# A hybrid transformer block on one core: the V products of softmax attention taken one key tile at a time, with two exp buffers and a 4 KB descriptor scratch

## The chip, the core and the metric

The kernel runs on one NeuronCore of a Trainium2 chip. The core has five engines, each with its own queue that is worked in order: TensorE (PE, the matrix multiplier, fed from SBUF and writing to PSUM), VectorE (DVE), ScalarE (ACT), GpSimd (POOL) and SyncE (SP, which here issues DMAs only). They meet through semaphores. The metric is the device time of the whole program in microseconds (us); lower is better. The bound used for "faster", "same" and "slower" is 0.2% of the time before, 7.4 us.

## The reference

The input x has 8 sequences of 512 tokens and 1024 channels. Four blocks follow one another, each on the layer-normed x and added back to x:

- softmax attention with 32 heads of 32 channels: q, k, v from one 1024x3072 weight, scores of all 512x512 token pairs per head, softmax over the keys, times v, then a 1024x1024 output product;
- a dense layer of 1024x1024 whose output is masked by a query mask and a row mask, both from a softmax over 64 cluster centroids;
- causal attention with a sigmoid in place of the softmax, 4 heads of 256 channels;
- the same masked dense layer again.

```python
scores = jnp.einsum('bhqd,bhkd->bhqk', q, k) * scale
probs = jax.nn.softmax(scores, axis=-1)
ctx = jnp.einsum('bhqk,bhkd->bhqd', probs, v)
```

All is float32. The change touches the first block alone.

## The kernel before

Everything is in one program whose order was written out by hand: each engine works its instructions in the order in which the Python code emits them, and the tile framework adds only the semaphore waits that the data need.

**Units.** The first block is worked in 64 units. Unit n is one sequence (n // 8) and one group of four heads (n % 8): four heads of 32 channels fill 128 partitions. For each unit the kernel needs q and k (128 channels x 512 tokens), v (4 key tiles of 128 tokens x 128 channels), the maximum of each score row, exp of the shifted scores, their sum over the keys, the products with v, and a division.

**The loop** (lines 1039 to 1107) has four steps, i = 0 to 3, for each unit n, and does in each step work for three units at once:

- `rows_step(n + 1, i)` (line 895): scores of the next unit with the queries on the partitions, into the four-bank PSUM tile `sc`, and a DVE reduction for the row maxima (L906);
- `between()` (line 986): filler, see below;
- in step 0 `turn_max(n)`: the maxima are turned with matmuls (`tpm`);
- `keys_step(n, i)` (line 928): scores of unit n for key tile i with the keys on the partitions, again into `sc`, preceded by a product with ones that puts the shift in (L934, L937), and then exp by ACT into the SBUF tile `pT` (L939);
- `values_step` (line 952): the products of `pT` with v, added up over the four key tiles in the PSUM tile `av` (L961). Before the change one call does two key tiles: the call for tiles 0 and 1 stands in step 2 after `keys_step(n, 2)`, the call for tiles 2 and 3 stands in step 0 of the next unit after `keys_step(n + 1, 0)`;
- in step 0, after that, `normalize(n - 1)` (line 965): the matmul `den` (L973) adds the exp sums over the partitions, DVE turns, inverts and multiplies (L976 to L981), ACT adds the bias (L982);
- `sum_step` (line 942): the sum of `pT` over the key tiles. POOL adds tiles 0 and 1 after the exp of tile 1 (L948, two instructions); DVE adds tile 2 in step 3, before `keys_step(n, 3)`, and tile 3 in step 0 of the next unit, behind the reduction (L950);
- a second `between(False, ...)`.

**Buffers around the change.** `sc` has one buffer, so rows and keys take turns in it: a `rows_step` waits for the exp before it, a `keys_step` for the reduction before it. `av` has one buffer, which the L981 of the unit before must have read. The small PSUM tiles `mm` (which also hold `den`, `tpm` and `logitsT`) have three. `pT` has three buffers of 8 KB a partition (pool `a_pt`, line 439): the exp of a key tile waits until the tile three before it has been read by its V products and by its sum.

**Filler.** The q, k and v projections of unit n + 2, the output products of an earlier sequence and the dense layer's cluster products are cut into pieces and queued; `Filler.take` (line 115) runs a share of the queue at each `between`, by the weights in `FILLER_SHARES` (line 39): three shares in step 0 (0.5, 0.5, 0.6), two in each of steps 1 to 3 (1.0 and 1.0; 0.6 to 1.0). What is left is run at the end of the unit (`filler.until`, line 1107). V products aren't filler and don't enter the shares. DVE gets side tasks (layer-norm statistics, sums for the fast matrix products: L241, L612, L752, L991, L1377) at the same places.

**Column form of the filler.** `product` (line 574) cuts each 128-column product into `P // width[0]` matmuls on neighbouring column groups of the array, two of 64 columns or four of 32, which run side by side. `between` sets the width with its second argument (line 993), and it holds until the next `between`. Filler after a `values_step` runs with 32 columns (the form of the V products), all other filler of the loop with 64. In the profile a matmul's form is written as rows\*columns of the array that it uses: 128\*64, 128\*32; the score products are 32\*64 (rows) and 32\*128 (keys). An fp32 matmul shows as two records.

**DMA.** SP issues the weight loads (six buffers of 256 KB, refilled as they are used). POOL issues the stores of intermediate results (188 DMAs in all). Their descriptors are kept in an SBUF scratch, whose size the program's constructor takes (line 1716); where nothing is said it is 16 KB a partition.

Of the kernel before, what the change touches and what calls it, by code (L numbers as in the profile page):

```python
# [26 lines left out]
TPB = S // P  # L27
NTILE = NT // P

HEADS_A, HD_A = 32, 32  # L30
GH = P // HD_A
# [42 lines left out]
class Filler:  # L74
# [47 lines left out]
    def run(self, count):  # L122

        while self.queue and count:
            count -= self._run_one() > 0
# [295 lines left out]
def softmax_attention(tc, cst, stage, filler, clusters, pools, dr, late, args):  # L421
# [11 lines left out]
    nc, small, ps_m = tc.nc, stage.small, stage.ps_m  # L433
    outer, inner = pools
# [1 line left out]
    fixed, ctxp, rpool, npool = outer("a_fixed", 1), outer("a_ctx", 2), outer("a_r", 3), outer("a_n", 1)  # L436
    owpool, csp, xTp, sump = outer("a_ow", OW_BUFS), outer("a_cs", 1), inner("a_xT", 2), inner("a_sum", 1)
    wpool, xpool = inner("a_w", W_BUFS), inner("a_x", 2)
    qkpool, vpool, ptp, tmp = inner("a_qk", 3), inner("a_v", 5), inner("a_pt", 3), inner("a_tmp", 1)
    shiftp, ps_s, ps_a = inner("a_shift", 2), inner("a_ps_s", 1, PSUM), inner("a_ps_a", 1, PSUM)  # L440

    qkvb_s = fixed.tile([P, 3 * NC], F32, name="qkvb_s")
# [7 lines left out]
    units, half = B * NC, NC // 2  # L450
# [220 lines left out]
    def left_tasks(b):  # L671

        xT = xTs[b]
        a11, a12, a21, a22 = (xT[:, ts(k, half), ts(m, 2 * P)] for m in range(2) for k in range(2))
        sums = (sump.tile([P, half, 2 * P], F32, tag=f"s{k}", name=f"s{k}_{b}") for k in (1, 2, 4))
        lefts[b], steps = left_sums(nc, a11, a12, a21, a22, *sums)
        return [lambda: run(enumerate(steps[:2])), *steps[2:]]
# [60 lines left out]
    def ow_sum_tasks(c):  # L738

        st = {}  # L740

        def load():
            for name in ("B11", "B12", "B21", "B22"):
                st[name] = owpool.tile([P, S], F32, tag="ow", name=f"ow_{name}_{c}")
                nc.sync.dma_start(st[name], ow_source(name, c))

        def step(k):
            if k == 0:
                t = [csp.tile([P, half, P], F32, tag=f"c{m}", name="cbox").rearrange("p c t -> p (c t)") for m in range(4)]
                st["t"] = (t[0], t[1], t[3], t[2])  # L750
                st["steps"] = right_sums(nc, st["B11"], st["B12"], st["B21"], st["B22"], *t)
            st["steps"][k]()  # L752
            nc.gpsimd.dma_start(dr.osums[("T1", "T2", "T4", "T3")[k]][:, ts(c, S)], st["t"][k])

        return load, [partial(step, k) for k in range(4)]
# [139 lines left out]
    def rows_step(n, qt):  # L895

        st = state[n]
        if qt == 0:
            st["nmax"] = small.tile([P, TPB, GH], F32, tag="nmax", name=f"nmax_{n}")
        sc = ps_s.tile([P, GH, S], F32, tag="sc", name="sc")  # L900
        for h in range(GH):
            rows = ts(h, HD_A)
            for j in range(2):
                cols = ts(2 * qt + j, P // 2)
                nc.tensor.matmul(sc[ts(j, P // 2), h, :], st["q"][rows, cols], st["k"][rows, :], start=True, stop=True)  # L905
        nc.vector.tensor_reduce(st["nmax"][:, qt, :], sc, AX.X, ALU.max, negate=True)  # L906
# [11 lines left out]
    def turn_max(n):  # L918

        st = state[n]  # L920
        tp = ps_m.tile([P, TPB, P], F32, tag="mm", name="tpm")
        for qt in range(TPB):
            part = parts[n % 2][:, qt, :, :].rearrange("p h c -> p (h c)")
            product(tp[:, qt, :], part, cst.ident_h, start=True, stop=True)
        st["shift"] = shiftp.tile([P, S], BF16, tag="shift", name=f"shift_{n}")
        nc.scalar.copy(st["shift"], tp.rearrange("p t q -> p (t q)"))
# [15 lines left out]
    def sum_step(n, kt):  # L942

        st = state[n]
        if kt == 1:
            st["sum"] = tmp.tile([P, GH, S], F32, tag="sum", name="sum")
            for h in (slice(0, GH // 2), slice(GH // 2, GH)):
                nc.gpsimd.tensor_tensor(st["sum"][:, h, :], st["pT", 0][:, h, :], st["pT", 1][:, h, :], ALU.add)  # L948
        else:
            nc.vector.tensor_tensor(st["sum"], st["sum"], st["pT", kt], ALU.add)  # L950

    def values_step(n, k):

        st = state[n]
        if k == 0:
            st["av"] = ps_a.tile([P, S], F32, tag="av", name="av")
        for kt in (2 * k, 2 * k + 1):
            pT = st.pop(("pT", kt))
            for h in range(GH):
                rows = ts(h, HD_A)  # L960
                nc.tensor.matmul(  # L961
                    st["av"][rows, :], st["v"][:, kt, rows], pT[:, h, :], start=(kt == 0), stop=(kt == TPB - 1)
                )

    def normalize(n):

# [19 lines left out]
    def between(sides=True, form=2 * HD_A):  # L986


        if sides:
            for _ in range(-(-len(side) // places[0])):  # L990
                side.popleft()()  # L991
            places[0] -= 1
        width[0] = form
        filler.take()

    def mix_tile(near, wait):
        norm, logits = tiles.popleft()(blocks=wait)
        filler.mix(norm[:2], 0 if near else 2, 2 if near else 5)
        filler.mix(norm[2:], 9 if near else 14, 3)
        if wait:  # L1000
            waiting.append(logits)
        elif near:
            filler.mix(logits[:1], 16, 4)
            carried.extend(logits[1:])
        else:
            filler.mix(logits, 22, 4)

    def weave(pieces, products):

        out, at = [], 0  # L1010
        for j, product in enumerate(products):
            upto = 2 * round(len(pieces) * (j + 1) / (len(products) + 1) / 2)
            out += pieces[at:upto] + product
            at = upto
        return out + pieces[at:]
# [23 lines left out]
    for n in range(units):  # L1039
        b, g = divmod(n, NC)  # L1040
        ahead = n + 2
        if n == NC - 2:
            weights.fill(W_BUFS)
        if n == NC:
            run(next(outs))
            ows.fill(OW_BUFS)
        count = 0
        if n > NC:
            count = OUT_SHARES[(n - 1) % half] if n <= units - NC else LAST_SHARES[n - units]
        products = [next(outs) for _ in range(count)]  # L1050
        if ahead < units:
            if g == NC - 2:
                side.extendleft(reversed(left_tasks(b + 1)))
            filler.add(weave(project_pieces(ahead), products), mark=ahead)
        else:
            filler.add(weave([], products))
        ready.extend(waiting)
        waiting.clear()
        if tiles:
            mix_tile(n == units - 1, ahead < units)  # L1060
        side.extend(ow_later)
        ow_later.clear()
        if n == NC - 1:
            side.extend(last_sums)
        for c in OUT_SUMS.get(n, ()):
            load, steps = ow_sum_tasks(c)
            side.append(load)
            (ow_later if c == 0 else side).extend(steps)
        if b + 1 < B:
            if g == 0:  # L1070
                norms = deque(norm_tasks(b + 1))
            if g < 2:
                run(enumerate(norms.popleft()))
            if norms:
                side.extend(norms.popleft())
        side.extend(held)
        held.clear()
        filler.plan(FILLER_SHARES)
        places[0] = TPB + 1
        for i in range(TPB):  # L1080
            if n + 1 < units:
                rows_step(n + 1, i)
            if i == 0 and n > 0:
                sum_step(n - 1, TPB - 1)
            between()
            if i == 0:
                turn_max(n)
                between()
            if i == TPB - 1:
                sum_step(n, i - 1)  # L1090
            keys_step(n, i)
            if i == 1:
                sum_step(n, i)
            if i == 0 and n > 0:
                values_step(n - 1, 1)
                if ready:
                    by_cluster, by_token = ready.popleft()
                    run([by_cluster])
                    filler.mix([by_token], 6, 1)
                normalize(n - 1)  # L1100
            if i == 2:
                values_step(n, 0)
            between(False, HD_A if i in (0, 2) and n > 0 else 2 * HD_A)
        if n + 1 < units:
            split_max(n + 1)
        if ahead < units:
            filler.until(ahead)
# [3 lines left out]
    tiles.clear()  # L1111
    run(ready[0][0][:1])
    del ready[0][0][0]
    values_step(units - 1, 1)
    normalize(units - 1)
    yield
    spare = Slices(ctxp.tile([P, NC, S], F32, tag="ctxT", name="spare").rearrange("p c t -> p (c t)"))
# [607 lines left out]
```

## Time and profile before

| | |
|---|---|
| time, median of 3 runs | 3715.86 us (3714.45 to 3716.66) |
| the profiled execution, from the first to the last instruction | 3715.1 us, 0.8 us (0.02%) under that median |
| mean granted TensorE clock | 0.999 |
| PE busy | 3677.4 us, 99% |
| DVE busy | 2539.7 us, 68% |
| ACT busy | 927.8 us, 25% |
| POOL busy | 594.9 us, 16% |
| the 64 units | 72.7 to about 2521 us of the span |
| HBM traffic | 160 GB/s over the span |

A busy share is a union of intervals, and the ends of matmuls are modelled from a pipeline, so a PE that is 99% busy can still lose time between two forms of matmul or in a wait that is shorter than the pipeline's tail. The starts of the records are the safer guide: where two stretches of matmuls start tells how long the first took. In a timeline line the columns are the start in us from the span's start, the length in us, the engine, the source line, the operation, output<-inputs, the form and output size, the number of records merged, and in brackets how long the engine had been idle and what ended that.

### The profile page before, as it was taken

The page shows a single profiled execution, that of the slowest core. Times are in us where ns is not written, and L with a number is a line of the kernel's source. Part 1 is how long each engine was busy: PE and PEld are TensorE (multiplying, and loading weights), DVE is VectorE, ACT ScalarE, POOL GpSimd, SP SyncE. Part 2 cuts the span into 40 slices and gives each one's busy share as a digit, 9 for nine tenths or more (in the row PEclk, how much of TensorE's full clock was granted, in tenths as well). Part 3 has the DMA queues.
Part 4 walks back from the last instruction along what each step waited for, and adds up shares of the span by engine and source line. Part 5 has one row for each costly group of instructions (what it writes and reads, how often), then busy time and mean ns, then how long its engine had stood idle before and what let it go on. Part 6 is the DMA issues. An engine that isn't in the chain of part 4 may idle for free.

```text
span 3715.1 us, 76365 instructions
## 1 busy us (share of the span) xinstructions
PE 3677.4 (99%) x32792; PEld 1876.7 (51%) x32792; DVE 2539.7 (68%) x3497; ACT 927.8 (25%) x1017; POOL 594.9 (16%) x574
## 2 busy tenths in 40 slices
PE   8999999999999999999999999999999999999999
PEld 4444544544545455445445445444444467774444
DVE  4777676767667677766767767666788845556656
ACT  1222222222222222222222222222111144430000
POOL 1222111111111111111111111111000044530000
PEclk9999999999999999999999999999999999999999
DMA  5335444645655555465465454347566767763332
GB/s 184 113 122 179 142 143 147 192 138 157 185 153 150 159 162 163 133 198 152 139 182 159 143 150 124 122 156 244 158 180 179 184 186 234 222 220 127 133 132 98
DMA packets 728641, 598.55 MB, mean 161 GB/s; under 512 B 322152, under 2 KB 574064, under 8 KB 728304
## 3 DMA queue, kind: packets, MB, share of 16 engines
q1 hardware_dynamic: 701072, 496.40, 46.6%
q0 software_dynamic: 22912, 81.54, 5.7%
q10 hardware_dynamic: 4320, 15.73, 1.0%
q8 instruction: 259, 4.24, 0.5%
q14 instruction: 78, 0.64, 0.0%
HBM read 459.30 MB, written 134.25 MB: 160 GB/s over the span
## 4 chain that ended last, share of the span: by engine, by line
PE 95%; DVE 3%; DMA 1%; issue 1%; ACT 0%; POOL 0%; SPq 0%; DVEq 0%; ACTq 0%; POOLq 0%
PE mm L578 42%; PE dense L1285 20%; PE sc L905 7%; PE av L961 6%; PE sc L937 6%; PE csc L1347 4%; PE o L1366 4%; PE sc L934 2%; PE logitsT L339 1%; PE den L973 1%; PE tp L291 1%; DVE nmax L906 1%; DVE sum L950 1%; PE tpm L578 0%; DVE s L1377 0%
## 5 line engine op out<-in xcount | busy, mean ns | idle before, releaser
L906 DVE TENSOR_REDUCE nmax<-sc 128x4 f32<-128x2048 f32 x256 | 586.0, 2289 | 295.3 <-PE sc L905 295.2
L939 ACT ACTIVATE pT<-sc 128x2048 f32<-128x2048 f32 x256 | 480.8, 1878 | 1122.3 <-PE sc L937 1122.3
L948 POOL TENSOR_TENSOR sum<-pT,pT 128x1024 f32<-128x1024 f32 x128 | 309.4, 2438 | 750.0 <-ACT pT L939 678.1
L578 PE MATMUL mm<-xT,w 128*64 128x256 f32 (+1 forms) x3736 | 428.1, 383 | 0.0
L578 PEld LDWEIGHTS mm<-xT,w 128*64 128x64 f32 (+1 forms) x3736 | 241.5, 135 | 204.1 <-issue 54.3
L578 PE MATMUL mm<-s,w 128*32 128x256 f32 (+1 forms) x3672 | 321.2, 381 | 1.2 <-DVE qk L158 1.2
L950 DVE TENSOR_TENSOR sum<-sum,pT 128x2048 f32<-128x2048 f32 x128 | 292.0, 2281 | 0.9 <-ACT pT L939 0.9
L905 PE MATMUL sc<-qk,qk 32*64 32x512 f32 x4096 | 285.1, 613 | 0.5 <-ACT pT L939 0.4
L156 DVE TENSOR_TENSOR u<-dense,u 128x512 f32<-128x512 f32 x223 | 148.0, 685 | 184.7 <-PE dense L1285 169.3
L578 PEld LDWEIGHTS mm<-s,w 128*32 128x32 f32 (+1 forms) x3672 | 180.4, 122 | 180.4 <-issue 68.9
L937 PE MATMUL sc<-qk,qk 32*128 32x512 f32 x2048 | 263.7, 589 | 0.0
L578 PE MATMUL mm<-ow,ctxT 128*32 128x512 f32 (+2 forms) x1276 | 247.2, 599 | 3.0 <-DMA ow<-o_T 2.8
L961 PE MATMUL av<-pT,v 128*32 128x512 f32 x2048 | 246.4, 598 | 0.2 <-ACT pT L939 0.2
L1285 PE MATMUL dense<-sum,s 128*128 128x512 f32 x512 | 231.8, 593 | 0.0
L578 PEld LDWEIGHTS mm<-w,xT 128*64 128x64 f32 (+1 forms) x3888 | 197.5, 133 | 62.2 <-issue 48.9
L578 PE MATMUL mm<-w,xT 128*64 128x128 f32 (+1 forms) x3888 | 218.1, 274 | 0.0
L158 DVE SCALAR_TENSOR_TENSOR qk<-mm,qkvb_s,qk 128x256 f32<-128x256 f32 x224 | 107.6, 480 | 123.2 <-PE mm L578 119.2
L1285 PE MATMUL dense<-wT_s,dT_b 128*128 128x512 f32 x384 | 171.2, 593 | 0.0
L1285 PE MATMUL dense<-wT_s,dT_a 128*128 128x512 f32 x384 | 171.2, 593 | 0.0
L578 PE MATMUL mm<-ow,c 128*64 128x512 f32 (+2 forms) x864 | 169.9, 596 | 0.2 <-DMA ow<-in_ow 0.2
L578 PE MATMUL mm<-w,s 128*64 128x128 f32 x2688 | 162.5, 274 | 0.0
L578 PEld LDWEIGHTS mm<-w,s 128*64 128x64 f32 x2688 | 148.0, 137 | 22.9 <-issue 22.9
(236 smaller groups left out, 4468.8 us busy)
## 6 DMA issues: line engine op xcount, KB each, us to landing
w<-in_qkvw SPq DMA_DIRECT2D x252, 256.0 KB, 3.0
ow<-o_T SPq DMA_DIRECT2D x240, 256.0 KB, 3.6
w<-qk_T SPq DMA_DIRECT2D x224, 256.0 KB, 2.8
ow<-in_ow SPq DMA_DIRECT2D x180, 256.0 KB, 3.3
w<-v_T SPq DMA_DIRECT2D x112, 256.0 KB, 2.7
x<-in_x SPq DMA_DIRECT2D x32, 512.0 KB, 5.3
dT_a<-xT SPq DMA_DIRECT2D x32, 512.0 KB, 5.7
x_a<-x SPq DMA_DIRECT2D x32, 512.0 KB, 6.5
```

Of the source, the lines that this page charges most:

```text
L156: nc.vector.tensor_tensor(out, acc, other, ALU.add)
L578: nc.tensor.matmul(out[cols], lhsT[:, cols], rhs, **flags)
L905: nc.tensor.matmul(sc[ts(j, P // 2), h, :], st["q"][rows, cols], st["k"][rows, :], start=True, stop=True)
L906: nc.vector.tensor_reduce(st["nmax"][:, qt, :], sc, AX.X, ALU.max, negate=True)
L937: nc.tensor.matmul(sc[:, h, :], st["k"][rows, ts(kt, P)], st["q"][rows, :], start=False, stop=True)
L939: nc.scalar.activation(pT, sc, AF.Exp, scale=SCALE_A)
L948: nc.gpsimd.tensor_tensor(st["sum"][:, h, :], st["pT", 0][:, h, :], st["pT", 1][:, h, :], ALU.add)
L950: nc.vector.tensor_tensor(st["sum"], st["sum"], st["pT", kt], ALU.add)
L961: nc.tensor.matmul(st["av"][rows, :], st["v"][:, kt, rows], pT[:, h, :], start=(kt == 0), stop=(kt == TPB - 1))
L1285: nc.tensor.matmul(st["acc"], st["left"][LEFT[k]][:, c, :], self.w[RIGHT[k]][:, c, :], start=(c == 0), stop=(c == half - 1),)
L1347: nc.tensor.matmul(sc[:, AT_OFF[i] : AT_OFF[i] + n], k[:, c, ts(i, P)], xT[:, c, i * P :], start=(c == 0), stop=(c == 1),)
L1366: nc.tensor.matmul(acc[:, j - jj, :], at[:, start : start + P], self.v[b * TPB + i][:, cols], start=(i == 0), stop=(i == j),)
```

## The change

The V products are called for one key tile at a time. The call for key tile i - 1 stands in step i, after `keys_step(n, i)`, for i = 1 to 3; that of key tile 3 stands in step 0 of the next unit, before the cluster product and `normalize`. So each of the four steps has one key tile of V products, where steps 0 and 2 had two each. The second `between` of every step runs its filler with 32 columns (but in step 0 of the first unit). The pool of the exp tiles has two buffers in place of three. The descriptor scratch is set to 4096 bytes a partition.

```diff
-    qkpool, vpool, ptp, tmp = inner("a_qk", 3), inner("a_v", 5), inner("a_pt", 3), inner("a_tmp", 1)
+    qkpool, vpool, ptp, tmp = inner("a_qk", 3), inner("a_v", 5), inner("a_pt", 2), inner("a_tmp", 1)
...
-    def values_step(n, k):
+    def values_step(n, kt):

         st = state[n]
-        if k == 0:
+        if kt == 0:
             st["av"] = ps_a.tile([P, S], F32, tag="av", name="av")
-        for kt in (2 * k, 2 * k + 1):
-            pT = st.pop(("pT", kt))
-            for h in range(GH):
-                rows = ts(h, HD_A)
-                nc.tensor.matmul(
-                    st["av"][rows, :], st["v"][:, kt, rows], pT[:, h, :], start=(kt == 0), stop=(kt == TPB - 1)
-                )
+        pT = st.pop(("pT", kt))
+        for h in range(GH):
+            rows = ts(h, HD_A)
+            nc.tensor.matmul(
+                st["av"][rows, :], st["v"][:, kt, rows], pT[:, h, :], start=(kt == 0), stop=(kt == TPB - 1)
+            )
...
             if i == 0 and n > 0:
-                values_step(n - 1, 1)
+                values_step(n - 1, TPB - 1)
                 if ready:
                     by_cluster, by_token = ready.popleft()
                     run([by_cluster])
                     filler.mix([by_token], 6, 1)
                 normalize(n - 1)
-            if i == 2:
-                values_step(n, 0)
-            between(False, HD_A if i in (0, 2) and n > 0 else 2 * HD_A)
+            if i > 0:
+                values_step(n, i - 1)
+            between(False, HD_A if i > 0 or n > 0 else 2 * HD_A)
...
-    values_step(units - 1, 1)
+    values_step(units - 1, TPB - 1)
     normalize(units - 1)
...
-    nc = bacc.Bacc("TRN2", target_bir_lowering=False, num_devices=1)
+    nc = bacc.Bacc("TRN2", target_bir_lowering=False, num_devices=1, dynamic_dma_scratch_size=4096)
```

## The prediction

> **What bounds the kernel now.** I read the page first: the busy times, then the chain that ended last.
>
> ```profile
> PE 3677.4 (99%) x32792; PEld 1876.7 (51%) x32792; DVE 2539.7 (68%) x3497; ACT 927.8 (25%) x1017; POOL 594.9 (16%) x574
> ...
> PE 95%; DVE 3%; DMA 1%; issue 1%; ACT 0%; POOL 0%; SPq 0%; DVEq 0%; ACTq 0%; POOLq 0%
> ...
> L939 ACT ACTIVATE pT<-sc 128x2048 f32<-128x2048 f32 x256 | 480.8, 1878 | 1122.3 <-PE sc L937 1122.3
> ```
>
> PE is the bound and DVE the only other engine on the chain. ACT waits for PE before nearly every exp. So the change is worth what it does to PE's order, less or more what PE then waits for. Next the PE rows of the timeline for steps 1 and 2 of a middle unit.
>
> ```profile
> 1226.36 1.03 PE L937 MATMUL sc<-qk,qk 32*128 32x512 f32 x8
> 1227.31 1.08 PE L578 MATMUL mm<-ow,c 128*64 128x512 f32 x4
> 1228.22 1.90 PE L578 MATMUL mm<-xT,w 128*64 128x256 f32 x16
> 1229.95 1.03 PE L578 MATMUL mm<-s,w 128*64 128x256 f32 x8
> 1230.91 1.11 PE L905 MATMUL sc<-qk,qk 32*64 32x512 f32 x16
> ...
> 1235.78 1.03 PE L937 MATMUL sc<-qk,qk 32*128 32x512 f32 x8
> 1236.74 1.92 PE L961 MATMUL av<-pT,v 128*32 128x512 f32 x16
> 1238.48 2.76 PE L578 MATMUL mm<-ow,c 128*32 128x512 f32 x24
> 1241.17 1.11 PE L905 MATMUL sc<-qk,qk 32*64 32x512 f32 x16
> ```
>
> Read the starts. Two records of 64 columns or four of 32 run side by side; call such a set a pass. In steady stretches passes start 0.429 us apart for 512 moving columns, 0.216 for 256 and 0.109 for 128, in both forms. Step 2: 4 + 6 passes of 512 are 4.29 us, the stretch takes 1241.17 - 1236.74 = 4.43, so 0.14 goes to the changes of form. Step 1: 2 of 512 and 12 of 256 are 3.45, the stretch takes 3.60: 0.15. The array is never short of work here. Two key tiles of V products take 1.74 (1238.48 - 1236.74), one takes 0.87.
>
> **PE's work.** (a) The V products: the same 2048 records, moved. (b) Changes of form: now steps 1 and 3 go keys (32\*128), filler (128\*64), rows (32\*64), and steps 0 and 2 keys, V and filler (128\*32), rows. I counted 125 stretches of the first kind and 124 of the second. After the change all are of the second kind: as many changes of form as before, each 0.015 us cheaper (medians 0.155 and 0.140 over nominal): 2 x 62 x 0.015 = 1.9 us gained. A rule to weigh here: the Trainium skill, TensorEngine Tiling (Array Packing), Tiling Modes, Key Properties, says that a change of tiling mode drains the engine, which speaks against calling the V products twice as often. By the row a drain is some 0.15 us; a reader who counts two added mode changes a unit by that rule would add 2 x 62 x 0.15 = 19 us, but the last line of the loop's edit moves the filler behind them into the same form. (c) Filler in 32 columns: 4,816 records of the loop (3,152 of them with 128 moving columns) become about 9,600, with as many weight loads. At equal pass time that costs nothing; its cover is the array's own streaming. The densest stretch shown is 16 passes of 128 columns at 0.110 us each, twice, and mostly 8 at 0.112. Step 3 will have 24 in a row (now 48 records at 64 columns, 2.77 us from start to start). If instructions then came only as fast as that stretch shows (96 records and loads in 2.77 us, 29 ns each), the last 8 passes would take 1.85 in place of 0.87, 1 us a unit, 62 us in all: the upper end. Below nothing: the 0.015 us of (b) is in already. I take nothing, nearest to the 16-pass runs.
>
> **What is moved, and which queue meets it.** Against now, everything on PE from the V products of step 0 to those of step 1 comes 0.87 us earlier, and from those of step 2 to those of step 3; the rest keeps its place. A wait of PE in these two windows that doesn't move with PE costs 0.87 less its slack. I took the slack of every wait there (PE's start less the time its semaphore was reached). No DMA wait that the semaphores date is within 2 us. exp before rows: 1.5 us or more in steps 0 and 2, 0.6 left. `av` is free 1.3 us or more before the keys of step 1 end, 4 to 6 as a rule. What is tight is DVE in step 0. The timeline of a unit in which DVE is behind:
>
> ```profile
> 1214.58 1.22 DVE L1377 TENSOR_TENSOR s<-xT 128x1024 f32<-128x1024 f32 x1
> ...
> 1214.79 1.92 PE L961 MATMUL av<-pT,v 128*32 128x512 f32 x16
> 1215.84 1.23 DVE L1377 TENSOR_TENSOR s<-s,xT 128x1024 f32<-128x1024 f32 x1
> ...
> 1216.54 1.06 PE L339 MATMUL logitsT<-nT,cT_s 128*32 128x128 f32 x32
> ...
> 1216.98 1.22 DVE L991 TENSOR_TENSOR xT<-xT 128x1024 f32<-128x1024 f32 x1
> ...
> 1217.41 1.04 PE L973 MATMUL den<-sum,ones 128*32 128x512 f32 x8
> ...
> 1218.12 0.48 DVE L158 SCALAR_TENSOR_TENSOR qk<-mm,qkvb_s,qk 128x256 f32<-128x256 f32 x1
> ...
> 1218.65 1.93 PE L578 MATMUL mm<-s,w 128*32 128x256 f32 x32 [0.20 <-DVE qk L158]
> ```
>
> PE reaches its first filler after `den` and waits for an `mm` buffer that L158 must empty; L158 stands behind three side tasks of 1.22 us, none of which waits for the V products. The second half of the V products was cover. With it gone PE comes 0.87 earlier and waits 0.87 longer, and the half that moved to step 1 still has to be run there. That is lost. It happens once for each sequence from the second to the seventh (at 588, 903, 1218, 1534, 1849 and 2165 us; the group's whole idle time is 1.2 us = 6 x 0.20): 6 x 0.87 = 5.2 us.
>
> The same in the first units, where keys of step 1 follow the reduction by 0.05 to 0.25 us: with the DVE room before that reduction subtracted, units 2 and 4 lose 0.3 each, unit 5 0.6, units 6 and 7 0.85 each (in both DVE has no gap since the step began): 2.9 us. In unit 62 0.3.
>
> The other way: at the start of twelve middle units (10, 12, 18, 20, 26, ... 52) PE waits now for DVE at `tpm` and again at the keys of step 0, some 0.15 us in all. DVE's queue there goes back to step 3's reduction, which moves 0.87 earlier: 12 x 0.15 = 1.8, say 2 us gained with unit 62. It also takes away two losses that the slack alone would give: `den` behind the DVE sum (slack 0.77 in units 10, 12, 20, ...) and L158 in units 18, 26, ... (0.72).
>
> **Two exp buffers.** The exp of key tile 2 now waits for POOL's sum of tiles 0 and 1 (two of 2.4 us, 4.8 in all, started 0.14 after the exp of tile 1), that of tile 3 for V products of the step before, those of the next unit for DVE sums that ended 5 us or more before. Exp 2 starts 0.87 us or more after POOL's end in units 0 to 8, 2.4 as a rule, and the V products added in step 1 widen that by 0.87. So nothing; the cover is a whole step of PE. In the last unit there are no rows and the steps are short:
>
> ```profile
> 2507.92 0.40 PE L934 MATMUL sc<-shift,ones_h 32*128 32x512 bf16 x4 [0.69 <-ACT pT L939]
> ...
> 2511.32 4.82 POOL L948 TENSOR_TENSOR sum<-pT,pT 128x1024 f32<-128x1024 f32 x2 [6.74 <-ACT pT L939]
> ...
> 2512.95 1.88 ACT L939 ACTIVATE pT<-sc 128x2048 f32<-128x2048 f32 x1 [0.70 <-PE sc L937]
> ...
> 2517.06 0.40 PE L934 MATMUL sc<-shift,ones_h 32*128 32x512 bf16 x4
> ```
>
> There exp 2 will wait until 2516.2 and end at 2518.1, and the keys of tile 3 start at 2518.2 in place of 2517.1: 1.1 us lost (it takes in the 0.87 at 2507.92).
>
> **The scratch.** POOL's queue moves 22,912 packets in 188 DMAs, 122 each, 8 a DMA engine. Shown at most: eight issued 0.6 us apart from 65.0 us on, about 4 us to landing, so 7 in flight. From zero (they fit) to POOL issuing one at a time: then in the eight units of the first sequence up to four issues before the sum would each take 4 in place of 0.6, the sum 14 us late, the exp behind it some 10: 80 us. I take zero, since POOL is idle 84% of the span and all but the first sequence issues one or two a unit. The Trainium skill, DMA: Bandwidth & Descriptors, Terms, gives 16 bytes for a descriptor; 4096 bytes are then an estimated 256 a ring. The freed SBUF is given to nothing.
>
> **Sum.** Losses 5.2 + 2.9 + 0.3 + 1.1 = 9.5; gains 1.9 + 2.0 = 3.9; net 5.6 us slower on a span of 3715.1, which is 0.8 under the median: 3721.5, rounded to 3721, 0.15% slower than the median before. About 0.2%, 7.4 us, is what a measurement of this kernel can tell from no change, so this is "same".
>
> **Rivals.**
> 1. DVE gives nothing back: 9.5 lost and the two struck losses on top (seven `den` of 0.13, five L158 of 0.18: 1.8), without the 2.0: 9.5 + 1.8 - 1.9 = 9.4, about 3725. For it: DVE is full from start to end of many steps. Against: its idle gap before step 3's reduction in those units (3.9 us at 728 us).
> 2. The 32-column filler of step 3 is short of instructions (slower; 3,152 records are 1,576 passes, so it decides alone from 7.4 / 1576 = 0.005 us more a pass, 0.114 us): up to 62 us on top of the main case, 3783; half of it, 3752, is more likely than all. For it: no stretch of that length is shown. Against: the two 16-pass runs.
> 3. Two buffers bind in the loop: exp 2 late in units 0 to 8 by up to 1 us if POOL slips, and rows after it: 5 to 10 us more, 3729.
> 4. The cheaper form and the evener spread win and DVE's waits vanish: 1.9 + 3.9 (all that the outliers of the 64-column stretches add up to) gained against the six waits and the last unit, 6.3: 3716.
> 5. The scratch binds: 80 us on top, 3801.
>
> **From cases to numbers.** Main case 0.45, between 3717 and 3723. Rival 1 0.17, rival 2 0.13, rival 3 0.06, rival 4 0.10, rival 5 0.02; 0.07 for a gain beyond 7.4 us that I can't place. Rival 1 ends slower by the bound (9 us), as do 2, 3 and 5: 0.38; faster 0.07; same 0.55. The range reaches from 3712 (rival 4 with the noise of the runs) to 3740 (rivals 1 and 3, and the lower third of rival 2); the main case alone would be 3717 to 3723.
>
> **What would show it.** Right: V products in four groups of 8 records a unit, the PE stretch after keys taking nominal plus 0.14 in all steps; PE idle before L578 from DVE L158 of about 1.06 in six places; the keys of step 1 in unit 6 idle 3.2 in place of 2.3; exp 2 of the last unit released by POOL; total records near 86,000. Wrong: passes of 128 columns above 0.114 us in step 3; exp starts released by POOL before 2500 us; POOL's DMA issues longer than 0.6 us; or `den` waiting for the sum in many units.

## The result, and the profile after

| | before | after |
|---|---|---|
| median of 16 runs each | 3715.40 us (3711.58 to 3718.64) | 3723.31 us (3721.05 to 3727.83) |
| ratio | | 1.0023, 95% interval 1.0015 to 1.0030 |
| the profiled execution, first to last instruction | 3715.1 us | 3724.4 us (its own time 3726.16, 2.9 over the median) |
| DVE busy | 2539.7 us | 2557.4 us |

The change costs 8 us (5.6 to 11.1 by the interval), which is clear of no change. The forecast of 3721 and its range hold. The likeliest sign, "same", stays open: the median lies 0.5 us past the bound of 7.4 us, and the interval takes the bound in. From the page of the kernel after (busy times, the chain that ended last, the exp's group):

```profile
PE 3675.9 (99%) x37608; PEld 1863.2 (50%) x37608; DVE 2557.4 (69%) x3497; ACT 926.6 (25%) x1017; POOL 599.0 (16%) x574
...
PE 93%; DVE 4%; DMA 1%; issue 1%; ACT 0%; POOL 0%; SPq 0%; DVEq 0%; POOLq 0%; ACTq 0%
...
L939 ACT ACTIVATE pT<-sc 128x2048 f32<-128x2048 f32 x256 | 481.0, 1879 | 1145.2 <-PE sc L937 1087.8
```

There are 4,816 more PE records, as counted, and PE is busy a little less than before. So PE has no more to do; it waits. On the chain DVE has 4% where it had 3%. DVE is busy 18 us longer with the same 3497 instructions, so some of them take longer. The groups of PE with the shapes kept apart say which waits grew. Before:

```profile
L578 PE MATMUL mm<-s,w 128*32 128x256 f32 x1968 | 119.2, 379 | 1.2 <-DVE qk L158 1.2
L934 PE MATMUL sc<-shift,ones_h 32*128 32x512 bf16 x1024 | 101.0, 384 | 5.9 <-DVE nmax L906 4.7 <-ACT pT L939 0.7
```

After:

```profile
L578 PE MATMUL mm<-s,w 128*32 128x256 f32 x2624 | 159.7, 379 | 6.5 <-DVE qk L158 6.4
L934 PE MATMUL sc<-shift,ones_h 32*128 32x512 bf16 x1024 | 101.3, 385 | 11.8 <-DVE nmax L906 9.2 <-ACT pT L939 2.3
```

The columns behind the bar are busy us, mean ns of one, and the idle time of PE just before them with what ended it. The filler's wait for L158 grew by 5.2 us, that of the keys for the row maxima (L906) by 4.5, and that for the exp by 1.6, all of it in the last unit. The first was foreseen to the tenth. Of the second 3.4 us lie in units 59 and 62 and weren't.

**Unit by unit.** The starts of the keys (L934) can be compared between two traces. The shift that builds up from step 0 of one unit to step 0 of the next is what that unit lost:

| units | predicted | after against before |
|---|---|---|
| all: 32-column form | -1.9 | -0.02 to -0.03 each, -1.7 |
| 0 | none | 0.7: V products of key tile 2 now run in its step 3 (0.87); in return step 0 of the last unit has one key tile fewer |
| 14, 22, 30, 38, 46, 54: L158 in step 0 | 5.2 | 0.88 each above the form's gain, 5.3 |
| 2, 4, 5, 6, 7 | 2.9 | 0.23, 0.23, 0.23, 0.87, 0.59 above the form's gain: 2.2 |
| relief of DVE in the middle units | -2.0 | 13 units, 0.04 to 0.34 each beyond the form's gain: -2.7 |
| 59 | none | **3.3** |
| 62 | 0.3 | **1.5** |
| the last (step 0 to step 3) | 1.1 | 0.9 |
| 10 and 26 | none | 0.5 and 0.6, PE waits there for output weights (a DMA) |

The sum is 10.6. The terms that the prediction had make 4.0 of it; units 59 and 62 make 4.8, unit 0 0.7 and the DMA waits 1.1. One profile can't tell a cost of the change from an accident of its execution, so the experiments had to: units 59 and 62 above all. (Ahead of unit 0, where the programs are alike, profiled executions differ by up to 3.5 us; the comparisons by unit leave that out.)

One of the six waits in the timeline of the kernel after, step 0 of unit 30 (start us, length us, engine, line; in brackets the idle time before and what ended it):

```profile
1216.94 1.22 DVE L1376 TENSOR_TENSOR s<-xT 128x1024 f32<-128x1024 f32 x1
1217.13 1.06 PE L960 MATMUL av<-pT,v 128*32 128x512 f32 x8
...
1218.20 1.23 DVE L1376 TENSOR_TENSOR s<-s,xT 128x1024 f32<-128x1024 f32 x1
1218.89 1.04 PE L972 MATMUL den<-sum,ones 128*32 128x512 f32 x8
...
1219.34 1.22 DVE L990 TENSOR_TENSOR xT<-xT 128x1024 f32<-128x1024 f32 x1
1220.47 0.48 DVE L158 SCALAR_TENSOR_TENSOR qk<-mm,qkvb_s,qk 128x256 f32<-128x256 f32 x1
...
1221.01 1.93 PE L578 MATMUL mm<-s,w 128*32 128x256 f32 x32 [1.08 <-DVE qk L158]
```

DVE's queue is as it was; PE arrives one key tile earlier and waits 1.08 in place of 0.20.

The last unit of the kernel after. The first line is the keys of step 1, the last those of step 3, and between them exp 2 starts when POOL's sum ends:

```profile
2515.95 0.40 PE L934 MATMUL sc<-shift,ones_h 32*128 32x512 bf16 x4 [1.49 <-ACT pT L939]
...
2519.35 4.76 POOL L948 TENSOR_TENSOR sum<-pT,pT 128x1024 f32<-128x1024 f32 x2 [6.68 <-ACT pT L939]
...
2524.14 1.88 ACT L939 ACTIVATE pT<-sc 128x2048 f32<-128x2048 f32 x1 [2.86 <-POOL sum L948]
...
2526.07 0.40 PE L934 MATMUL sc<-shift,ones_h 32*128 32x512 bf16 x4 [0.78 <-ACT pT L939]
```

There are two losses here. At step 1 PE waits 1.49 for exp 0 where it waited 0.69: the V products that left step 0 were cover, and the 0.87 that unit 0 spends on them is not won back. At step 3 it waits 0.78 for exp 2, where it didn't wait.

Unit 59, before and after. Before:

```profile
2360.64 1.88 ACT L939 ACTIVATE pT<-sc 128x2048 f32<-128x2048 f32 x1 [3.53 <-PE sc L937]
...
2361.97 0.68 DVE L785 TENSOR_TENSOR c<-ctxT 128x512 f32<-128x512 f32 x1
2362.65 5.25 POOL L948 TENSOR_TENSOR sum<-pT,pT 128x1024 f32<-128x1024 f32 x2 [31.59 <-DVE c L785]
2362.69 2.93 DVE L785 TENSOR_TENSOR c<-c,ctxT 128x512 f32<-128x512 f32 x1
...
2365.54 2.28 DVE L906 TENSOR_REDUCE nmax<-sc 128x4 f32<-128x2048 f32 x1
...
2367.87 0.40 PE L934 MATMUL sc<-shift,ones_h 32*128 32x512 bf16 x4 [0.86 <-DVE nmax L906]
```

After:

```profile
2363.09 1.88 ACT L939 ACTIVATE pT<-sc 128x2048 f32<-128x2048 f32 x1 [3.53 <-PE sc L937]
...
2365.10 5.21 POOL L948 TENSOR_TENSOR sum<-pT,pT 128x1024 f32<-128x1024 f32 x2 [31.57 <-ACT pT L939]
2365.28 2.77 DVE L785 TENSOR_TENSOR c<-ctxT 128x512 f32<-128x512 f32 x1
...
2368.08 2.78 DVE L785 TENSOR_TENSOR c<-c,ctxT 128x512 f32<-128x512 f32 x1
...
2370.79 2.28 DVE L906 TENSOR_REDUCE nmax<-sc 128x4 f32<-128x2048 f32 x1
...
2373.12 0.61 PE L934 MATMUL sc<-shift,ones_h 32*128 32x512 bf16 x4 [2.82 <-DVE nmax L906]
...
2373.50 1.95 PE L937 MATMUL sc<-qk,qk 32*128 32x512 f32 x8
```

Before, the first L785 is done when POOL's sum begins, and only the second is long (2.93). After, the V products stand between exp 1 and the filler of step 1, so that filler and the DVE work behind it come one tile later against exp 1; both L785 fall beside the sum and take 2.8 us each. The reduction behind them is late, and PE idles 2.82. Then comes a second loss: eight records of L937 that take 1.03 elsewhere take 1.95. The table by window of the kernel after (stretch, its length, PE busy with records, granted clock, DMA share, GB/s) says why:

```profile
2372.00:2374.00 2.00, 0.88 (x8) 0.67 0.03 10
2374.00:2376.00 2.00, 2.00 (x12) 0.50 0.00 0
2376.00:2378.00 2.00, 2.00 (x36) 0.98 0.00 0
```

From the last part of the long wait on the granted clock is 0.50, for 3.4 us in all.

### The profile page after: what moved, and what is told of

Read it like the earlier page. It is cut to its first block, busy times and chain, and to the rows that moved or that the text cites. A ratio compares the mean times of both kernels' runs of the same rounds, so it can differ in the third digit from the quotient of the medians.

```text
span 3724.4 us, 85960 instructions
## 1 busy us (share of the span) xinstructions
PE 3675.9 (99%) x37608; PEld 1863.2 (50%) x37608; DVE 2557.4 (69%) x3497; ACT 926.6 (25%) x1017; POOL 599.0 (16%) x574
## 4 chain that ended last, share of the span: by engine, by line
PE 93%; DVE 4%; DMA 1%; issue 1%; ACT 0%; POOL 0%; SPq 0%; DVEq 0%; POOLq 0%; ACTq 0%
PE mm L578 40%; PE dense L1284 20%; PE sc L905 7%; PE av L960 6%; PE sc L937 6%; PE o L1365 4%; PE csc L1346 4%; PE sc L934 2%; PE logitsT L339 1%; PE den L972 1%; DVE nmax L906 1%; DVE sum L950 1%; PE tp L291 1%; DMA ow<-o_T 1%; DVE box L612 0%
## 5 line engine op out<-in xcount | busy, mean ns | idle before, releaser
L906 DVE TENSOR_REDUCE nmax<-sc 128x4 f32<-128x2048 f32 x256 | 585.9, 2289 | 259.0 <-PE sc L905 258.1
L578 PE MATMUL mm<-xT,w 128*32 128x256 f32 (+1 forms) x4832 | 426.8, 381 | 0.3 <-DVE rden L975 0.3
L578 PEld LDWEIGHTS mm<-xT,w 128*32 128x32 f32 (+1 forms) x4832 | 236.8, 123 | 206.1 <-issue 37.8
L960 PE MATMUL av<-pT,v 128*32 128x512 f32 x2048 | 273.9, 607 | 0.2 <-ACT pT L939 0.2
L937 PE MATMUL sc<-qk,qk 32*128 32x512 f32 x2048 | 264.3, 590 | 0.0
L578 PEld LDWEIGHTS mm<-w,xT 128*32 128x32 f32 (+1 forms) x5440 | 199.2, 119 | 57.7 <-issue 44.4
L578 PE MATMUL mm<-w,xT 128*32 128x128 f32 (+1 forms) x5440 | 217.0, 273 | 0.0
L158 DVE SCALAR_TENSOR_TENSOR qk<-mm,qkvb_s,qk 128x256 f32<-128x256 f32 x224 | 107.4, 479 | 124.2 <-PE mm L578 120.2
L578 PE MATMUL mm<-ow,c 128*32 128x512 f32 (+2 forms) x928 | 170.4, 594 | 0.7 <-DMA ow<-o_T 0.6
L578 PE MATMUL mm<-w,s 128*32 128x128 f32 (+1 forms) x4000 | 161.5, 273 | 0.0
L578 PEld LDWEIGHTS mm<-w,s 128*32 128x32 f32 (+1 forms) x4000 | 149.7, 119 | 18.4 <-issue 18.4
```

What stands on the lines that cost most here:

```text
L578: nc.tensor.matmul(out[cols], lhsT[:, cols], rhs, **flags)
L937: nc.tensor.matmul(sc[:, h, :], st["k"][rows, ts(kt, P)], st["q"][rows, :], start=False, stop=True)
L960: nc.tensor.matmul(st["av"][rows, :], st["v"][:, kt, rows], pT[:, h, :], start=(kt == 0), stop=(kt == TPB - 1))
```

## The experiments

My theory after the result: the losses are (1) cover gone from step 0, (2) in units 59 and 62 DVE operations held up by POOL's sum, with (3) a low clock after the wait; the buffers cost only the last unit, the scratch nothing. Rivals: the buffers or the scratch cost something in the loop; the finer V calls or the 32-column filler are dear in themselves; units 59 and 62 are an accident of one execution.

### Three exp buffers, default scratch

```diff
-    qkpool, vpool, ptp, tmp = inner("a_qk", 3), inner("a_v", 5), inner("a_pt", 2), inner("a_tmp", 1)
+    qkpool, vpool, ptp, tmp = inner("a_qk", 3), inner("a_v", 5), inner("a_pt", 3), inner("a_tmp", 1)
...
-    nc = bacc.Bacc("TRN2", target_bir_lowering=False, num_devices=1, dynamic_dma_scratch_size=4096)
+    nc = bacc.Bacc("TRN2", target_bir_lowering=False, num_devices=1)
```

> The V products, the calls and the 32-column filler as changed; the exp tiles have three buffers again and the scratch its default size. Theory (the moved V products make the loss, the buffers cost only the last unit's 1 us): about 1 us under the changed kernel, 3722, with the six waits for L158, unit 59's 3.3 us and unit 62's 1.5 us still there. Rival (two exp buffers or the small scratch make a good part of the loss in the loop): the time falls back by 4 us or more, towards 3715 to 3719, and units 59 and 62 lose nothing.

Measured: 3722.61 us, ratio to before 1.0024 (1.0015 to 1.0032). Every unit's shift is that of the kernel after to 0.03 us, with unit 59 at 3.6 and unit 62 at 1.5, except units 2 (0.2 more), 10 and 26 (no DMA wait this time) and the last (0.1 in place of 0.9). So the loss belongs to the order of the V products; the two buffers cost 0.8 us in the last unit, where exp 2 waits for POOL. In the times that 0.8 can't be seen (8.5 us over the kernel before here, 7.9 with two buffers). The keys of step 1 in the last unit wait 1.54 with three buffers too, so that loss is the order's. And units 59 and 62 are no accident of one execution.

### Only the scratch

```diff
-nc = bacc.Bacc("TRN2", target_bir_lowering=False, num_devices=1)
+nc = bacc.Bacc("TRN2", target_bir_lowering=False, num_devices=1, dynamic_dma_scratch_size=4096)
```

> The kernel before with the 4 KB descriptor scratch and nothing else. Theory (POOL's DMA issues never fill the ring): the kernel before, within 1 us, and every unit's keys start as before. Rival (the scratch binds in the first sequence, where up to four stores are issued before a sum): units 0 to 7 up to 10 us late each, 80 us in all.

Measured: 3714.52 us, ratio 0.9999 (0.9990 to 1.0008); every unit's shift is 0.00 or 0.01 but one (unit 6, -1.64: the kernel before had a low clock there in its profile, this execution hadn't). The scratch costs nothing.

### Only the 32-column form

```diff
-            between(False, HD_A if i in (0, 2) and n > 0 else 2 * HD_A)
+            between(False, HD_A if i > 0 or n > 0 else 2 * HD_A)
```

> The kernel before, V products in pairs as they were, with 32-column filler after the keys of all steps. Theory (a stretch with 32-column filler changes form 0.015 us cheaper, 124 stretches): 1.9 us faster than before, 3713.5, spread evenly over the units, 0.03 each; records as many as in the changed kernel. Rival (short 32-column passes of the filler are short of instructions in step 3): 5 to 60 us slower than before, with passes of 128 columns above 0.114 us. Rival (no difference by form): 3715.4.

Measured: 3713.37 us, ratio 0.9996 (0.9987 to 1.0005). By time it can't be told from the kernel before; in the trace 0.02 to 0.03 us are gained in nearly every unit, some 1.6 in all. Unit 10 lost 4.0 us in this execution, waiting for output weights, with the old order of the V products: so that wait doesn't need the new order. The passes of 128 columns (four of the 3,712 records to a pass) are as dense as in the kernel before:

```profile
L578 PE MATMUL mm<-w,xT 128*32 128x128 f32 x3712 | 110.2, 273 | 0.0
```

110.2 us for 3712 / 4 passes is 0.119 each with the tail of every stretch; in 24-pass stretches of the kernel after they start 0.109 apart.

### The filler of steps 1 and 3 back in 64 columns

The edit of the form alone, undone in the kernel after, so that filler and V products differ in form in these steps.

```diff
-            between(False, HD_A if i > 0 or n > 0 else 2 * HD_A)
+            between(False, HD_A if i in (0, 2) and n > 0 else 2 * HD_A)
```

> The changed kernel with the filler after the keys of steps 1 and 3 in 64 columns again, so that 124 stretches go keys, V products in 32 columns, filler in 64, rows: one change of form more each. Theory (the 0.14 us of a stretch are two or three changes of about equal price, 0.05 to 0.07 each): 124 times 0.065 to 0.085, with the 0.015 of the form, 8 to 10.5 us over the changed kernel, 3731 to 3734. Rival (each change drains the array at the price of a whole stretch, 0.15): 19 us, 3742. Rival (a change between 32 and 64 columns with the same 128 rows is free): 1.9 us, 3725.

Measured: 3742.90 us, ratio 1.0072 (1.0060 to 1.0085), 18 us over the kernel after by the ratios, 19.6 by the medians (of two chips). My estimate was wrong and the dearest rival right. Step 1 of a middle unit, kernel after:

```profile
1229.67 1.07 PE L960 MATMUL av<-pT,v 128*32 128x512 f32 x8
1230.55 1.04 PE L578 MATMUL mm<-ow,c 128*32 128x512 f32 x8
...
1234.11 1.11 PE L905 MATMUL sc<-qk,qk 32*64 32x512 f32 x16
```

With 64 columns:

```profile
1238.64 1.07 PE L960 MATMUL av<-pT,v 128*32 128x512 f32 x8
1239.63 1.08 PE L578 MATMUL mm<-ow,c 128*64 128x512 f32 x4
...
1243.23 1.11 PE L905 MATMUL sc<-qk,qk 32*64 32x512 f32 x16
```

The same products take 4.59 in place of 4.44 us; the V products alone go from 0.88 to 0.99. Over nominal, the median of the V stretch is 0.138 and of the 64-column stretch behind it 0.155, where the joined stretch has 0.140: one change of form is 0.15 us, not a third or half of that. 124 x 0.153 = 19.0; the trace shows 0.30 more in nearly every unit, 18.8 up to the last one when the DMA waits of units 10 and 26 in the kernel after are left out. The line of the change that widens the 32-column form is worth more than twice what the whole change loses.

### Cover back in step 0

Key tiles 2 and 3 in step 0 as before, tiles 0 and 1 in steps 1 and 2, none in step 3; three buffers, default scratch, 32-column filler.

```diff
             if i == 0 and n > 0:
+                values_step(n - 1, TPB - 2)
                 values_step(n - 1, TPB - 1)
...
-            if i > 0:
+            if i in (1, 2):
                 values_step(n, i - 1)
```

> As the changed kernel, but step 0 keeps the V products of two key tiles (2 and 3 of the unit before), steps 1 and 2 have one key tile each and step 3 none; three exp buffers, default scratch. Theory (the loss in step 0 is cover of 0.87 us that went): the six waits for L158 fall back to 0.2 us each and the first units lose nothing, so the time is 7 us under the changed kernel by these parts; what units 59 and 62 lose by POOL's sum beside DVE stays where step 1 is as changed (4.8 us): 3714 to 3718. If that loss goes too, 3713. Rival (the loss is the finer calls themselves, or the 32-column form): 3721 to 3724, as the changed kernel.

Measured: 3716.72 us, ratio 1.0007 (0.9998 to 1.0015). From its trace, the same groups as above:

```profile
L578 PE MATMUL mm<-s,w 128*32 128x256 f32 x2624 | 159.7, 379 | 1.3 <-DVE qk L158 1.3
L934 PE MATMUL sc<-shift,ones_h 32*128 32x512 bf16 x1024 | 101.2, 385 | 9.4 <-DVE nmax L906 8.1 <-ACT pT L939 0.7
```

The six waits are back at 0.21 each, and units 3 to 7 and unit 0 lose nothing (unit 2 lost 0.5 in this execution; it lost 0.4 with the form alone, too, where the V products keep their old order). Units 59 and 62 lose 3.3 and 1.5, as in the kernel after, because step 1 is as changed. The two causes are apart: the first comes from step 0, the second from step 1.

### POOL's sum left out in units 59 and 62

```diff
         if kt == 1:
             st["sum"] = tmp.tile([P, GH, S], F32, tag="sum", name="sum")
+            if n in (59, 62):
+                nc.scalar.copy(st["sum"], st["pT", 0])
+                return
```

> The changed kernel, with POOL's sum of key tiles 0 and 1 left out in units 59 and 62 alone: ACT copies tile 0 into the sum there, so key tile 1 is missing from the denominators of these two units. Theory (in these units DVE operations with two SBUF inputs run beside POOL's sum and take 2.8 us in place of 0.7, and the row maxima come late): unit 59 gets back 3.3 us, unit 62 1.5 us, the L785 operations there take 0.7 us, 3718.5 in all. Rival (something else is late there, the DMA of an output weight or the filler's order): the two units lose as before, 3723. Rival (the loss in these units was of one execution only): the changed kernel's median doesn't hold it, and this kernel is within 1 us of it.

Measured: 3718.97 us, ratio 1.0011 (1.0003 to 1.0020), 3.6 us under the kernel with three buffers on the same chip, although this one has two, which cost 0.8 in the last unit. Unit 59 is 0.95 us shorter than in the kernel before, unit 62 even with it. Its timeline in unit 59:

```profile
2362.51 1.89 ACT L948 COPY sum<-pT 128x2048 f32<-128x2048 f32 x1
...
2362.93 0.68 DVE L785 TENSOR_TENSOR c<-ctxT 128x512 f32<-128x512 f32 x1
...
2363.64 0.69 DVE L785 TENSOR_TENSOR c<-c,ctxT 128x512 f32<-128x512 f32 x1
...
2365.32 2.29 DVE L906 TENSOR_REDUCE nmax<-sc 128x4 f32<-128x2048 f32 x1 [0.99 <-PE sc L905]
...
2367.88 0.40 PE L934 MATMUL sc<-shift,ones_h 32*128 32x512 bf16 x4
```

Without the sum the same operations take 0.68 and 0.69 us, and PE doesn't wait. So it is POOL's sum that holds them up. In the kernel before it held up one of the two; PE's wait of 0.86 there is most of the 0.95.

### PE kept busy in the two longest waits

Two unread matmuls, 1.7 us of PE, in the kernel after.

```diff
+            if (n, i) in ((6, 1), (59, 2)):
+                keep_busy(n, 2)    # tile = ps_m.tile(...); 2 x matmul(tile, cst.ident, state[n]["k"])
             keys_step(n, i)
```

> The changed kernel, with two matmuls of 512 columns whose result nobody reads (1.7 us of PE) put into the two longest waits, ahead of the keys of step 1 in unit 6 (PE idle 2.4 us) and of step 2 in unit 59 (2.8 us). Theory (the wait itself is set by DVE, but the granted clock falls to 0.50 for 3.4 us after it, 1.7 us lost each time): no stretch of clock 0.50 after either wait, units 6 and 59 about 1.7 and 1.4 us shorter, 3 us in all, 3720. Rival (the clock falls by chance, or with the power drawn, not because PE idles): the time of the changed kernel, 3723, or more by the added matmuls, and the clock falls as before.

Measured: 3723.45 us, ratio 1.0021 (1.0012 to 1.0031). In the trace it is as the theory has it: unit 6 is 1.64 and unit 59 1.38 us shorter, at the same windows the clock is full,

```profile
2372.00:2374.00 2.00, 1.62 (x4) 1.00 0.63 206
2374.00:2376.00 2.00, 1.47 (x16) 1.00 0.00 1
2376.00:2378.00 2.00, 2.00 (x36) 1.00 0.00 0
```

and the row maxima come no sooner: the keys behind both waits start as far into their units as without the added matmuls. So the wait is DVE's, and the low clock behind it is a cost of its own that follows from PE being idle, as far as one execution with two such places can show it. In the times it can't be seen: the gain of 3 us is as wide as the interval, and in the profiled execution units 10 and 26 lost 2.1 us more than in the kernel after, the two units whose wait for output weights varies from one execution to the next. That the total gains is not shown.

### A version from these parts

Three buffers, default scratch, 32 columns everywhere. Key tile 2 in step 3, but in step 0 of the next unit where that one needs cover; tiles 0 and 1 together in step 2 in units 59 and 62.

```diff
+    cover = {2, ..., 7, 14, 22, 30, 38, 46, 54}
+    def tiles_at(n, i):
+        if i == 0:
+            return (2, 3) if n + 1 in cover else (3,)
+        first = (0, 1) if n in (59, 62) else (1,)
+        return ((), () if n in (59, 62) else (0,), first, () if n + 1 in cover else (2,))[i]
...
-                values_step(n - 1, TPB - 1)
+                for kt in tiles_at(n - 1, 0):
+                    values_step(n - 1, kt)
```

> Three exp buffers, default scratch, 32-column filler in all steps. V products of key tile 2 in step 3, but in step 0 of the next unit (with tile 3) where that step needs cover: next units 2 to 7, 14, 22, 30, 38, 46, 54. Those of tile 0 in step 1, but in step 2 (with tile 1) in units 59 and 62, so that POOL's sum comes there as before. Theory, unit by unit from the runs so far: 1.9 us from the form, 2.7 from DVE's relief in units 9 to 57, 1.6 from unit 6, less 0.1 in the last unit: 6 us faster than before, 3708 on 3714.1. Rival (the parts get into each other's way, or the relief needs the moved tile everywhere): the form's 1.9 alone or less, 3712 to 3716.

Measured: 3711.50 us, ratio 0.9989 (0.9980 to 0.9998), 3.7 us faster than before and some 12 faster than the kernel after. Against the kernel before that is 0.1%, half of the bound, with an interval just clear of no change. The waits for L158 and for the row maxima are those of the kernel before, and the 0.8 more for the exp is in the last unit:

```profile
L578 PE MATMUL mm<-s,w 128*32 128x256 f32 x2624 | 159.7, 379 | 1.3 <-DVE qk L158 1.3
L934 PE MATMUL sc<-shift,ones_h 32*128 32x512 bf16 x1024 | 101.0, 384 | 6.6 <-DVE nmax L906 4.7 <-ACT pT L939 1.5
```

In the trace this kernel is 5.3 us shorter from the first keys to the last. 1.6 of that is unit 6 and no gain of the order: the profiled execution of the kernel before had a stretch of half clock there and this one hadn't. The 3.7 that are left are form and relief, about as expected, less the 0.9 that the V products moved out of the last unit's step 0 cost. I read the 0.56 by which unit 7 is longer as a loss. The same with unit 8 among the covered ones and two unread matmuls in unit 6:

> As the mixed order, with unit 8 among those whose step 0 gets two key tiles, and the two unread matmuls in unit 6's wait. Theory: 0.6 us from unit 8 against the mixed order (3711.5 on 3715.2), and the 1.7 us of the low clock in those executions in which it fell: 0.6 to 1.5 us less, 3710 to 3711 on 3715.2. Rival: unit 6's matmuls come late and cost up to 1 us, 3712 or more.

Measured: 3710.74 us, ratio 0.9991 (0.9982 to 0.9999). Unit 7 is as long as in the kernel before, but unit 8 is now 0.83 longer: what I had read as a loss in unit 7 was one more key tile of V products (0.87) that fell into that unit, and covering unit 8 only passes it on. So the 0.6 was not there to be won. There is no low clock in the loop; waits for weights in units 10 and 26 took 1.2 more in this execution. By time the two can't be told apart. Both are faster than the kernel before by some 0.1%.

## Why the prediction was right or wrong

- **PE's work, and the form (right).** Records and the stretch of 0.14 over nominal in all steps are as predicted, and the traces show 1.6 to 1.7 us gained against 1.9. Rival 2 is out: 24 passes in a row start 0.109 us apart. The rule of the Trainium skill that I weighed (TensorEngine Tiling (Array Packing), Tiling Modes, Key Properties: a change of tiling mode drains the engine) fits the runs, though they show the time of a change and not what the array does in it, and the 19 us that a reader would have got by it is what the run with 64 columns lost. I was right that the last edit avoids it.
- **Cover in step 0 (right).** 5.2 predicted, 5.3 in the trace, and giving the cover back took it away.
- **First units (mechanism right, sizes a little high).** 2.9 against 2.2: unit 5 lost 0.2 in place of 0.6, unit 7 0.6 in place of 0.85. The sign that I gave for unit 6 did not come: its keys of step 1 wait 2.40, not 3.2. The unit lost its 0.87 all the same, but in more places: PE waits 0.32 before these keys for DVE's L975, which empties an `mm` buffer, and the filler around it starts a little late as well.
- **DVE relief (right).** 2.0 against 2.7, in units 9 to 57. Rival 1 (DVE gives nothing back) is out, though its time, 3725, lies a little nearer to the median than mine: about the right size, from the wrong cause. Rival 4 (DVE's waits vanish) is out: they grew.
- **Two buffers (right).** Nothing in the loop; in the last unit exp 2 waits for POOL as foreseen, and the keys behind it come 0.9 late against 1.1. Rival 3 is out, and so is rival 5, the scratch.
- **What failed: "a wait of PE in these two windows that doesn't move with PE costs 0.87 less its slack".** The slacks were taken with DVE's operations at their durations of before. But the V products in step 1 also shift the filler of that step, and the DVE work that follows it, against exp 1 and so against POOL's sum. In units 59 and 62 that turned operations of 0.7 us into 2.5 to 2.8. It was shown by the run without these sums: 3.6 us by the times, 5.8 by the units' shifts (4.3 and 1.5), 0.95 of which the kernel before loses too. The timeline of before had the warning: one L785 of 2.93 us beside the sum.
- **A smaller failure: "the rest keeps its place".** In unit 0 nothing leaves step 0, so key tile 2 in its step 3 makes every later unit start 0.87 later. The last unit would give that back, but there PE waits for the exp, and the V products taken out of its step 0 were cover: the wait is 1.49 in place of 0.69. This term, 0.7 us in the trace with the form's gain in it, wasn't in the sum; the run with both key tiles in step 0 doesn't have it.
- **The sum of the prediction (low by the missing terms).** 9.5 - 3.9 = 5.6 predicted. What was predicted measured 4.0 and the terms that were missing 4.8 and 0.7: 9.5, against 7.9 (5.6 to 11.1) by the medians. That the point came within 3 us is owed in part to the other terms' being 1.6 too high. The table hides one more cost: in unit 6 both profiles have a low clock, but of the five traces with the shorter wait of before only two have it, of the four with the longer wait all four (last section). An estimate from these counts is 3/5 of 1.64, 1.0 us, that the change costs there on average.

## What to carry to other kernels

When work is moved, look not only at whose wait loses its cover but at which instructions of two engines now run at the same time: a row whose longest instance is four times its median marks a collision, and a shift of a microsecond can add another, by turning the instruction that started first into the one that waits. Give a moved stretch of matmuls the form of its neighbours; each change of form costs the array 0.15 us here. And place cover unit by unit where DVE is behind rather than evenly: the uneven order came out 0.1% faster than the paired one, the cheaper form included, and 0.3% faster than the even one. When work moves across units, ask also whether a longer unit lost time or only holds more work.

## What the runs showed of the hardware

**DVE beside POOL.** In the kernel after, beside POOL's sum (which reads SBUF) the operation `r<-ct,r`, both of whose inputs lie in SBUF, takes 2.48 us in the median (13 instances) and 0.69 elsewhere (32). Those with one input in PSUM, `ct<-mm,ct` (0.69 and 0.68) and L158 (0.483 both), the reduction L906 (2.29 and 2.29) and the transposes L308 (1.235 both) are not held up. The same 13 instances overlap POOL's sum in the kernel before and take 0.69. One of them, before:

```profile
440.75 0.69 DVE L788 TENSOR_TENSOR r<-ct,r 128x512 f32<-128x512 f32 x1
441.12 4.97 POOL L948 TENSOR_TENSOR sum<-pT,pT 128x1024 f32<-128x1024 f32 x2 [11.19 <-ACT pT L939]
```

After:

```profile
441.09 5.28 POOL L948 TENSOR_TENSOR sum<-pT,pT 128x1024 f32<-128x1024 f32 x2 [11.01 <-ACT pT L939]
441.58 2.50 DVE L788 TENSOR_TENSOR r<-ct,r 128x512 f32<-128x512 f32 x1
```

So an overlap is not enough: before, DVE's operation began 0.36 us ahead of POOL's (once 0.66) and POOL's instruction took the longer time (2.6 in place of 2.4 in 12 of the 13); after, POOL began 0.2 to 0.5 us ahead and DVE waited. The group in both kernels, before:

```profile
L788 DVE TENSOR_TENSOR r<-ct,r 128x512 f32<-128x512 f32 x45 | 29.8, 690 | 1.0
```

After:

```profile
L788 DVE TENSOR_TENSOR r<-ct,r 128x512 f32<-128x512 f32 x45 | 53.4, 1214 | 1.0
```

That is 23.6 us, more than all of what DVE has gained in busy time (17.7; L558, which meets the sum less often now, gives 5.1 back). By the shifts of the units, PE sees it in 59 and 62 alone. The Trainium skill, SBUF — State Buffer, SBUF: two separate sides, says it: a DVE operation with two SBUF inputs and a GpSimd operation that reads SBUF take turns at a shared port, for the whole instruction. The trace agrees: each long DVE operation ends some 0.55 us after the POOL instruction that was running when it began, and 0.55 is most of its usual length of 0.69, so little of it is done before.

**The clock after a wait.** In the loop the half clock always lasted 3.41 us; it cost 1.6 in unit 6 and 1.4 in unit 59 of the kernel after, where it began 0.4 us before the wait ended. With three buffers it began there 1.0 us behind the wait, and that unit is 0.3 us longer. In the nine profiled executions without added matmuls the wait of unit 6 shows 2.30 us five times, with a low clock behind it in two, and 2.40 us four times, with a low clock in all four. The waits of 2.6 to 2.8 us in unit 59 had it in all four, those of 1.2 to 1.6 us in units 62 and 63 never. Once it followed two waits for weights in a row, 1.21 and 0.84 us (32-column form alone, unit 10). The Trainium skill, TensorE: Matmul & The Clock Gate, Part 1, gives an idle window of some 3.4 us, free-running, as the condition: the length of the low clock agrees with that window, but here a wait of 2.4 us was enough, and 2.3 sometimes. What decides at 2.3 was not tried.
